# A two-layer graph network on one core: a new order for the first three and the last two graphs, and one seed of the last graph written straight into its own bank

## The chip, the cores and the metric

The kernel runs on one core of one Trainium2 chip. The metric is the device time of one execution in microseconds (us). PE (TensorE) does the matmuls, ACT (ScalarE), DVE (VectorE) and POOL (GpSimd) the elementwise work, SP (SyncE) issues every DMA. PSUM is used as eight banks of 128 partitions x 512 fp32 values, `bank0` to `bank7`.

## The reference, cut to what matters

64 graphs, each with `x` (256 nodes x 512 features) and an adjacency `adj` (256x256), all fp32:

```python
h = relu(layernorm(x))                                   # layer 0
agg = (adj @ h) / rowsum(adj)
x = x + relu(concat(h, agg) @ W.T)                       # W is 512 x 1024
h = relu(layernorm(x))                                   # layer 1
Xw = h @ Wv + bv
e = leaky_relu((Xw @ aw[:512]).T + Xw @ aw[512:] + ab)   # 256 x 256
T = adj * exp(e);  T = T / rowsum(T)
x = x + relu(h @ Wk[0] + bk[0] + (T @ h) @ Wk[1] + bk[1] + (T @ T @ h) @ Wk[2] + bk[2])
```

## The kernel before, in words

Matrix products are done with fewer block products than usual: Strassen-like sums of half-size blocks are prepared first (`wide` for W of layer 0, `main` for the rest, with steps numbered 1 to 7), and each block product is a 128x128 by 128x256 matmul, two recorded matmuls per fp32 block. All matmuls go through line 459, all bank-to-SBUF copies on ACT through line 471, the DVE sums with a bank operand through 474 and 477 (in `wide` through 652), the sums without one through `pool_op`, 420 on DVE or 422 on POOL.

One graph goes through the stages prepare (layer norm, adjacency scaled by its row sums), prepared, wide, layer0, turn1 (second norm and two vectors `sj`, `si`), transition (T), moved, once (T @ h), inner, turned1 and outer (the output). Stages of several graphs overlap; from the third graph on a transposed copy is made through DRAM (`put`, line 380, and `get`, line 386), for the first graphs on PE (`flip_on_pe`, line 404).

**What sets the order.** Every operation is registered by `add(engine, cost, run, reads, writes)` (line 231). Its place is a number: graph x `TURN` (38.52) plus the entry of the table `AT` for its stage, in order of registration, counted from 0. The stages `first` and `weights` belong to no graph and take the bare number. `emit` (line 253) sorts by this number, and what one engine got is that engine's instruction order; an instruction whose inputs are late holds back all that follow on its engine. `cost` is handed to `note` (line 250), which does nothing. The suffixes `_0`, `_1`, `_2` name the first three graphs, `_late` and `_last` the last two; the graphs between use tables without a suffix. Below, "transition_0.6" is operation 6 of stage transition of graph 0.

Operations that matter later:

- `first`: 0 and 1 load the halves of graph 0's x; 6 to 9 load the four 512 KB blocks of W into `x2` to `x5` (line 784); 10 to 24 (even) transpose it on PE (line 796), two blocks for each; the odd ones copy to SBUF on ACT; 27 to 54 are the 28 DVE sums that make W's block forms (lines 812 and 814); 55 to 57 load graph 0's adjacency, graph 1's x and graph 1's adjacency (lines 342, 345).
- `wide`: its PE operations use a form of W each; wide_0.16 is the first DVE sum (line 652) on a product of graph 0.
- layer0: 4 to 14 are products and seeds; 15 and 16 (line 563) finish x. turn1: 0 to 7 the norm, 8 to 11 `sj` and `si` on DVE (line 677), 13 and 14 DVE transposes, 15 to 18 the four writes of them to DRAM.
- transition: 0 writes `sj` to DRAM (line 686), 1 reads it back as a row (line 687), 2 to 5 are leaky ReLU and exp on ACT (692, 695), 6 and 7 the product with adj and its sums on DVE (697), 8 and 9 the reciprocal, 10 and 11 the scaling on ACT (703), 12 and 14 the PE transposes (404), 13 and 15 their copies (410).
- inner: 0 (step 1), 1 (step 7), 4 (step 2) and so on multiply `zg` with Wk[2]'s forms `lq`.
- outer of the last graph runs `main` with `last`: p, r, d are banks 3, 4, 5, x and y banks 6 and 7. Steps 5, 1, 6, 7 sum into bank 3; after each of them DVE adds a bias and puts the result as a "seed" into another bank (line 474 or 477), on which steps 2, 3 and 4 go on. The seed of step 3 goes into the upper half of bank 4, and after step 2 ACT copies it to bank 7 (line 546); step 3 waits for that. Each finished quarter of the output is added to x (line 756) and written (line 758).

Of the kernel before, what the change touches and what calls it, by code (L numbers as in the profile page):

```python
# [11 lines left out]
AF = mybir.ActivationFunctionType  # L12
# [15 lines left out]
    "first": (-90.93, -53.23, -117.99, -108.94, -110.36, -116.23, -69.23, -51.75, -160.39, -107.21, -61.21, -22.37, -27.53, -12.34, -45.26, -1.78,  # L28
        -84.29, -28.27, -93.32, 13.37, -47.15, -20.43, -156.60, -71.50, -119.21, -46.84, -42.27, -129.45, -122.63, -61.71, -52.35, -32.94, -72.67,
        -62.56, -45.91, -151.57, -67.52, -60.72, 2.83, 15.02, -11.78, 19.40, 29.16, -47.95, -25.77, 48.23, -47.81, -32.81, -19.46, -48.89, 7.13,  # L30
        20.41, -32.63, 17.85, 10.53, -123.51, 5.76, 21.86),
    "inner": (105.13, 108.59, 106.23, 109.69, 109.89, 110.76, 112.05, 116.38, 111.97, 114.07, 117.47, 117.50, 122.79, 115.08, 117.06, 118.02, 137.51),
    "inner_0": (104.64, 107.10, 112.63, 109.63, 108.85, 109.21, 114.17, 115.99, 113.73, 110.41, 129.80, 114.72, 119.54, 110.75, 113.34, 116.02,
        129.11),
    "inner_1": (110.70, 112.22, 111.49, 112.47, 113.83, 115.31, 114.08, 115.66, 116.33, 115.18, 129.29, 117.74, 125.91, 116.89, 117.80, 117.56,
        155.03),
    "inner_2": (110.70, 111.20, 111.98, 113.63, 111.78, 114.32, 114.94, 116.88, 115.46, 116.06, 116.42, 116.98, 124.86, 117.74, 119.04, 117.57,
        134.35),
    "inner_last": (336.53, 367.29, 384.59, 334.45, 391.73, 454.67, 522.64, 533.37, 408.60, 470.37, 504.02, 528.93, 492.30, 558.54, 500.07, 537.12,
        580.23),  # L40
    "inner_late": (108.31, 111.76, 110.85, 113.85, 112.13, 112.69, 114.05, 114.68, 123.33, 115.61, 145.82, 118.27, 122.89, 115.88, 119.11, 120.04,
        164.89),
    "layer0": (20.96, 24.01, 34.26, 38.15, 36.30, 37.47, 38.90, 39.56, 40.20, 40.90, 41.49, 42.16, 41.93, 42.79, 43.22, 43.47, 44.25),
    "layer0_0": (43.30, 43.73, 40.76, 63.15, 62.04, 64.91, 63.69, 65.17, 65.45, 66.86, 68.03, 68.37, 68.31, 69.19, 69.32, 68.45, 68.75),
    "layer0_1": (31.27, 36.57, 33.97, 43.43, 46.13, 48.74, 46.62, 49.21, 46.86, 49.66, 48.01, 49.83, 48.25, 48.79, 50.67, 49.93, 50.78),
    "layer0_2": (24.88, 28.19, 23.22, 43.47, 37.98, 37.09, 39.47, 39.22, 40.19, 41.59, 40.57, 42.04, 42.75, 43.10, 41.23, 47.00, 44.33),
    "layer0_last": (50.01, 57.68, 33.91, 60.79, 65.66, 66.71, 68.41, 66.94, 69.01, 68.24, 69.91, 69.27, 70.80, 71.03, 72.73, 71.96, 75.23),
    "layer0_late": (15.20, 21.71, 35.30, 40.31, 42.84, 48.47, 47.89, 49.57, 47.98, 49.76, 48.90, 49.94, 48.91, 50.48, 49.70, 51.70, 50.97),
    "loads": (-59.49, -45.29),
    "loads_2": (-40.12, -36.06),  # L50
    "loads_last": (-58.91, -32.90),
    "loads_late": (-54.89, -85.13),
    "moved": (89.04, 92.46, 93.17, 93.66, 94.15, 98.50),
    "moved_0": (94.08, 96.00, 97.15, 96.58),
    "moved_1": (87.63, 93.34, 94.62, 96.56, 97.69, 105.10),
    "moved_2": (88.68, 91.56, 91.23, 91.84, 96.02, 106.19),
    "moved_last": (139.05, 163.46, 205.96, 169.91),
    "moved_late": (96.66, 97.72, 100.63, 101.15),
    "once": (61.25, 64.00, 75.09, 75.88, 94.29, 95.59, 94.96, 99.41, 98.19, 98.63, 100.80, 101.23, 101.56, 100.30, 105.75, 103.00, 102.97, 103.89,
        106.56, 107.35, 108.14),  # L60
    "once_0": (85.34, 86.38, 98.69, 87.50, 93.62, 98.46, 98.58, 97.73, 98.58, 100.34, 100.69, 102.20, 101.36, 98.56, 103.24, 103.33, 102.27, 102.98,
        104.33, 105.25, 108.42),
    "once_1": (57.59, 69.48, 97.24, 96.50, 95.31, 95.58, 95.01, 99.66, 97.26, 98.27, 100.29, 102.15, 100.46, 102.80, 103.34, 105.40, 106.15, 108.95,
        105.21, 110.88, 111.17),
    "once_2": (63.41, 76.25, 69.81, 96.68, 93.52, 97.13, 93.09, 100.30, 100.95, 102.43, 103.05, 103.30, 102.21, 102.90, 103.59, 109.13, 104.57,
        107.39, 107.54, 109.97, 115.46),
    "once_last": (102.80, 135.83, 148.28, 162.89, 124.41, 120.18, 145.98, 187.50, 162.35, 203.89, 212.10, 233.57, 187.89, 213.05, 223.02, 232.11,
        256.18, 243.42, 255.25, 267.18, 321.27),
    "once_late": (66.99, 88.23, 64.29, 90.92, 99.96, 101.37, 100.45, 101.19, 101.37, 101.90, 105.80, 107.13, 110.31, 103.81, 110.60, 107.37, 105.93,
        106.50, 106.70, 107.63, 115.35),  # L70
    "outer": (108.93, 110.52, 122.87, 129.37, 114.22, 117.68, 119.41, 120.07, 120.70, 121.57, 122.87, 123.53, 124.60, 125.46, 126.33, 126.99, 127.62,
        130.65, 131.52, 132.19, 128.92, 131.95, 134.55, 134.99, 141.93, 152.31, 138.02, 140.19, 162.69, 160.60, 164.14, 164.93),
    "outer_0": (94.35, 98.74, 125.62, 106.70, 102.31, 116.27, 117.12, 118.24, 117.50, 117.80, 121.31, 124.46, 124.00, 125.58, 126.52, 126.71, 128.22,
        128.87, 132.65, 133.67, 128.80, 131.21, 134.36, 137.61, 140.55, 144.44, 136.33, 141.49, 160.49, 160.36, 163.66, 166.03),
    "outer_1": (106.89, 111.90, 118.77, 120.53, 108.75, 117.68, 119.18, 119.21, 120.59, 120.95, 123.23, 122.93, 123.75, 126.63, 126.70, 127.43,
        127.87, 128.74, 130.19, 132.33, 130.44, 131.84, 139.05, 141.13, 148.79, 152.10, 133.45, 136.68, 160.29, 160.80, 164.22, 166.72),
    "outer_2": (108.39, 111.96, 127.91, 140.81, 108.40, 121.23, 123.19, 121.63, 124.71, 125.64, 126.27, 125.65, 128.28, 128.68, 129.01, 128.91,
        131.04, 134.92, 135.36, 134.36, 132.23, 135.69, 137.94, 142.17, 143.69, 152.32, 138.41, 140.22, 150.30, 161.80, 164.00, 171.57),
    "outer_last": (498.02, 668.57, 694.33, 671.17, 577.46, 581.61, 593.26, 565.87, 615.19, 623.17, 650.49, 630.60, 695.13, 726.44, 735.87, 784.68,
        743.01, 838.42, 843.34, 796.04, 842.17, 761.60, 792.50, 751.08, 788.70, 811.00, 818.37, 858.45, 840.44, 876.17, 953.80, 975.74, 975.14,  # L80
        1020.56, 876.63, 891.60, 907.44, 875.80, 872.80),
    "outer_late": (109.06, 117.31, 186.73, 151.51, 116.15, 116.30, 119.62, 120.47, 120.01, 120.90, 123.12, 123.38, 129.10, 132.52, 132.66, 129.78,
        134.77, 139.77, 140.44, 139.50, 141.87, 144.49, 145.13, 158.57, 188.07, 200.85, 150.49, 152.04, 158.47, 232.29, 199.18, 211.96),
    "prepare": (-43.06, -41.74, -40.72, -35.30, -36.24, -28.72, -27.19, -23.45, -19.80, -15.93, -24.36, -24.98, -20.94, -12.75, -1.76, -2.28, -14.82,
        -13.49, -12.68, -12.13, -11.03, -11.58, -0.32, 1.04, 0.48, 2.14, 1.59),
    "prepare_0": (-84.88, -53.30, -37.93, -28.72, -22.39, -78.13, -74.85, -6.63, -18.20, -7.49, -144.71, -60.68, -137.04, -101.76, -12.58, -21.22,
        -26.38, -2.11, -10.47, 18.05),
    "prepare_1": (-15.07, -17.62, -8.06, -6.13, -0.14, -1.19, -0.63, 0.54, 7.75, 18.63, -38.44, -18.61, -14.54, 4.73, 16.46, 7.28, 12.55, 17.02,
        21.02, 19.33),
    "prepare_2": (-29.75, -29.48, -28.24, -24.75, -27.62, -28.40, -18.19, -16.40, -14.88, -13.91, -13.33, -6.35, -3.17, 8.62, 7.51, 7.67, -7.58,  # L90
        -2.32, -3.08, -1.25, 10.97, -0.12, 9.45, 9.24, 6.13),
    "prepare_last": (-41.49, -47.42, -40.82, -36.74, -38.40, -39.37, -36.21, -27.41, -24.96, -22.93, -7.95, -5.29, -3.53, 0.52, -2.38, -0.41, -8.95,
        -8.06, 0.10, 9.16, 6.05, -3.83, 2.64, 1.68, 2.00, -1.88, -3.02),
    "prepare_late": (-34.61, -47.32, -24.01, -19.75, -22.44, -22.19, -20.22, -19.93, -12.10, -16.22, -28.31, -35.76, -26.99, -25.62, -0.63, -19.64,
        -11.10, -13.45, -13.43, -9.03, -11.19, -7.53, -0.35, -0.68, -1.43, -1.97, 0.33),
    "prepared": (-7.18, 5.89, 11.28),
    "prepared_0": (8.94, 11.22, 28.01, 44.28),
    "prepared_1": (30.89, 31.47, 31.46, 30.86),
    "prepared_2": (13.00, 25.59),
    "prepared_last": (9.25, 6.90, 2.69),  # L100
    "prepared_late": (-3.13, 0.63, 10.23),
    "transition": (52.39, 56.28, 64.51, 63.42, 65.05, 63.97, 66.52, 67.12, 67.73, 68.04, 68.40, 68.92, 69.51, 71.25, 71.80, 70.70, 72.35),
    "transition_0": (74.09, 74.94, 85.61, 86.74, 87.55, 87.22, 90.49, 90.24, 90.60, 91.41, 91.25, 92.03, 91.61, 91.53, 93.51, 94.10),
    "transition_1": (53.67, 62.32, 65.20, 65.85, 69.15, 70.70, 67.77, 67.85, 67.92, 69.48, 74.55, 74.24, 70.13, 70.67, 70.52, 71.81, 77.46),
# [5 lines left out]
    "turn1_1": (49.63, 49.70, 50.51, 51.10, 51.13, 51.73, 53.03, 53.21, 53.66, 53.93, 58.29, 58.86, 64.81, 54.56, 54.30, 58.29, 62.00, 58.02, 61.54),  # L110
    "turn1_2": (43.11, 45.01, 43.93, 52.82, 53.16, 53.50, 49.16, 51.40, 52.03, 52.20, 54.30, 57.90, 58.08, 51.29, 54.09, 59.58, 56.28, 52.52, 56.97),
    "turn1_last": (75.41, 78.96, 77.17, 178.47, 184.64, 192.21, 86.15, 103.27, 80.59, 81.84, 83.21, 85.38, 104.79, 93.44, 122.16, 115.84, 150.29,
        115.69, 113.30),
    "turn1_late": (42.12, 48.32, 51.63, 53.75, 53.93, 54.07, 55.81, 56.33, 52.09, 61.66, 67.71, 71.29, 74.60, 66.82, 79.34, 84.95, 89.16, 79.81,
        97.48),
    "turned1": (100.59,),
# [155 lines left out]
def gnn_two_layers(ctx: ExitStack, tc: tile.TileContext, x, adj, w0, wv, bv, aw, ab, wk, bk, out):  # L272
    nc = tc.nc
# [702 lines left out]
```

## Time and profile before

| | us |
|---|---|
| median of 3 runs | 2547.44 (2547.05 to 2548.68) |
| the profiled execution's own time | 2545.75 |
| its span | 2544.0 |
| PE busy in it | 2509.1 (99%), 12412 matmuls |
| DVE, ACT, POOL busy | 1653.6, 1322.6, 1560.1 |
| DMA moved | 296.85 MB, mean 117 GB/s |
| mean granted PE clock | 0.997 |

The profile has several views. The table by stretches gives for each window of time the busy time of every engine, the clock that PE was granted (1.00 is full speed) and the DMA load. The timeline lists instructions in order of time, merged where several alike follow one another: start, duration, engine, line of the kernel, what it writes and reads, how many, and in square brackets the idle time before it and who ended that. The chain is the sequence of work that ended last, followed back from the end. A matmul's end is modelled, so the distance between starts says more than one duration.

### The profile page before, as it was taken

What the parts mean: (1) busy time and instruction counts of PE and PEld (TensorE: products, weight loads), DVE (VectorE), ACT (ScalarE), POOL (GpSimd) and SP (SyncE); (2) the same over time, 40 slices, a digit from 0 to 9 for tenths busy, and PEclk for the clock granted to TensorE, in tenths of its full rate; (3) what the DMA queues carried; (4) which work ended last, traced back from release to release, by engine and by line L of the source; (5) the groups of instructions that cost most, each with busy time, mean ns of one, the idle gap of its engine ahead of it and who ended that gap; (6) DMA issues with size and microseconds to landing.
All of it is one profiled execution on the core that took longest, in us unless ns stands there. A gap on an engine that the chain in (4) does not pass through costs nothing.

```text
span 2544.0 us, 39950 instructions
## 1 busy us (share of the span) xinstructions
PE 2509.1 (99%) x12412; PEld 2213.5 (87%) x12412; DVE 1653.6 (65%) x4099; ACT 1322.6 (52%) x3551; POOL 1560.1 (61%) x2475
## 2 busy tenths in 40 slices
PE   7899999999999999999999999999999999999998
PEld 5688888888888888888888888888888888888887
DVE  5766666666666666666666666666666666666654
ACT  7455555555555555555555555555555555555521
POOL 5565666666666666666666656656666666666640
PEclk9999999999999999999999999999999999999999
DMA  4354454454454454444444544544544544544421
GB/s 150 85 131 117 113 129 120 115 125 117 117 129 112 115 135 110 119 125 120 120 120 116 127 121 111 128 122 113 127 119 117 126 113 116 135 112 115 110 71 44
DMA packets 574571, 296.85 MB, mean 117 GB/s; under 512 B 417171, under 2 KB 540819, under 8 KB 574358
## 3 DMA queue, kind: packets, MB, share of 16 engines
q1 hardware_dynamic: 574358, 294.31, 47.0%
q8 instruction: 98, 1.61, 0.3%
q14 instruction: 115, 0.94, 0.1%
HBM read 162.80 MB, written 131.40 MB: 116 GB/s over the span
## 4 chain that ended last, share of the span: by engine, by line
PE 96%; DVE 1%; DMA 1%; SPq 0%; ACT 0%; issue 0%; POOL 0%; DVEq 0%; ACTq 0%; POOLq 0%
PE bank L459 96%; DMA dh<-turned 0%; DMA x<-in_L_gnn_W_dram 0%; DMA l<-in_L_gnn_Wv_dram 0%; SPq L380 0%; DVE bank L474 0%; DVE zg L420 0%; DMA out_dram<-x 0%; DVE z L677 0%; DVE turned L376 0%; PE bank L404 0%; ACT h1n L362 0%; DVE bank L652 0%; SPq L345 0%; DVE zg L474 0%
## 5 line engine op out<-in xcount | busy, mean ns | idle before, releaser
L459 PE MATMUL bank<-l,s 128*128 128x256 f32 x3292 | 876.9, 380 | 6.6 <-ACT bank L546 2.1
L459 PEld LDWEIGHTS bank<-l,s 128*128 128x128 f32 x3292 | 611.6, 191 | 91.4 <-issue 5.1
L471 ACT COPY stg<-bank 128x256 f32<-128x256 f32 x944 | 337.2, 371 | 524.8 <-PE bank L459 203.6
L459 PE MATMUL bank<-l,zg 128*128 128x256 f32 x1820 | 469.2, 380 | 1.6 <-ACT mz L471 0.9
L459 PE MATMUL bank<-lq,zg 128*128 128x256 f32 x1792 | 447.8, 380 | 3.7 <-DVE zg L474 1.3
L459 PEld LDWEIGHTS bank<-lq,zg 128*128 128x128 f32 x1792 | 340.4, 190 | 51.1 <-DVE zg L474 2.3
L459 PEld LDWEIGHTS bank<-l,zg 128*128 128x128 f32 x1820 | 337.2, 191 | 42.3 <-ACT mz L471 1.7
L422 POOL TENSOR_TENSOR zg<-zg 128x256 f32<-128x256 f32 x183 | 131.7, 733 | 353.8 <-ACT zg L471 347.4
L652 DVE TENSOR_TENSOR bank<-bank,stg 128x256 f32<-128x256 f32 x505 | 210.3, 428 | 202.1 <-PE bank L459 138.8
L459 PE MATMUL bank<-l,h0t 128*128 128x256 f32 x1008 | 291.3, 382 | 1.6 <-DVE q L652 0.8
L422 POOL TENSOR_TENSOR s<-h0t,s 128x256 f32<-128x256 f32 x315 | 234.0, 743 | 0.5
L459 PEld LDWEIGHTS bank<-l,h0t 128*128 128x128 f32 x1008 | 197.4, 197 | 26.8 <-DVE q L652 2.3
L677 DVE SCALAR_TENSOR_TENSOR z<-h1n,v_sb 128x512 f32<-128x512 f32 x256 | 211.9, 828 | 13.1 <-ACT h1n L368 4.4
L459 PE MATMUL bank<-l,h1t 128*128 128x256 f32 x784 | 203.3, 381 | 1.3 <-DVE lo L477 1.0
L471 ACT COPY qf<-bank 128x256 f32<-128x256 f32 x128 | 47.6, 372 | 285.3 <-DVE qf L474 250.3
L422 POOL TENSOR_TENSOR qf<-qf 128x256 f32<-128x256 f32 x122 | 113.5, 930 | 117.4 <-DVE qf L474 117.4
L459 PEld LDWEIGHTS bank<-l,h1t 128*128 128x128 f32 x784 | 153.1, 197 | 20.1 <-DVE lo L477 2.3
L563 DVE SCALAR_TENSOR_TENSOR x<-bank,x 128x512 f32<-128x512 f32 x254 | 165.4, 686 | 2.7 <-PE bank L459 1.9
L459 PE MATMUL bank<-q,sa 128*128 128x256 f32 x512 | 152.9, 380 | 2.3 <-DVE bank L474 1.6
L459 PE MATMUL bank<-qf,st 128*128 128x256 f32 x512 | 152.6, 380 | 0.8 <-DVE qf L420 0.7
L422 POOL TENSOR_TENSOR s<-h0t 128x256 f32<-128x256 f32 x189 | 143.5, 773 | 9.3 <-ACT h0t L410 6.6
L422 POOL TENSOR_TENSOR hf<-h1n,hf 128x256 f32<-128x256 f32 x124 | 91.3, 736 | 89.9 <-PE bank L459 89.9
(178 smaller groups left out, 4418.3 us busy)
## 6 DMA issues: line engine op xcount, KB each, us to landing
dh<-turned SPq DMA_DIRECT2D x500, 128.0 KB, 3.3
h1t<-dh SPq DMA_DIRECT2D x64, 512.0 KB, 3.8
x<-in_x_dram SPq DMA_DIRECT2D x63, 512.0 KB, 4.6
out_dram<-x SPq DMA_DIRECT2D x63, 512.0 KB, 3.1
h0t<-dh SPq DMA_DIRECT2D x61, 512.0 KB, 4.0
a<-in_adj_dram SPq DMA_DIRECT2D x64, 256.0 KB, 4.3
dan<-turneda SPq DMA_DIRECT2D x248, 64.0 KB, 1.9
raw<-dan SPq DMA_DIRECT2D x62, 256.0 KB, 2.7
```

What stands on the lines that cost most here:

```text
L422: add("POOL", cost, lambda: getattr(nc.gpsimd, f)(to, p, q), reads, writes)
L459: nc.tensor.matmul(ps, lhs, rhs, start=start, stop=True, skip_group_check=True)
L471: add("ACT", 0.37, lambda: nc.scalar.copy(dst, bank[b][:, cols]), [f"bank{b}"], dkeys)
L563: add("DVE", 0.75 if sums else 0.69, lambda c=c: nc.vector.scalar_tensor_tensor(t[:, c, :], bank[banks[1 + c]], 0.0, t[:, c, :], op0=ALU.m ...
L652: add("DVE", 0.43, lambda f=f, to=to, x=x, y=y: getattr(nc.vector, f)(to, x, y), pbk + [k], tok)
L677: add("DVE", 0.79, lambda s=s, c=c: nc.vector.scalar_tensor_tensor(scr.rearrange("p c n -> p (c n)"), h[:, c, :], 1.0, v_sb[:, s, :], op0= ...
```

## The change

Three things are edited. First, the tables for `first`, `weights` and all stages with the suffixes `_0`, `_1`, `_2`, `_late` and `_last` get new numbers; the tables without suffix, `TURN` and `SHIFT` stay. Second, in `main` with `last` the seed of step 3 is written by DVE to bank 7 at once, and ACT's copy is gone (the list for `outer_last` has one entry less, so its entries from 26 on move down by one). Third, three `cost` values of ACT operations with a row sum are larger. The changed file has one line more, so its line numbers above 528 are larger by one (and back by the removed lines where those lie).

```diff
-    "first": (-90.93, -53.23, -117.99, -108.94, -110.36, -116.23, -69.23, -51.75, -160.39, -107.21, -61.21, -22.37, -27.53, -12.34, -45.26, -1.78,
...
-        20.41, -32.63, 17.85, 10.53, -123.51, 5.76, 21.86),
+    "first": (-259.48, -286.32, -474.02, -306.06, -368.19, -123.55, -208.45, -206.90, -285.80, -358.64, -231.88, -223.99, -262.31, -253.20, -282.95,
...
+        -276.54, -348.24, -262.55, -227.12, -429.92, -242.38, -165.16, -204.46, -43.14, -159.19, -203.45, -533.74, -116.49),
...
-    "inner_0": (104.64, 107.10, 112.63, 109.63, 108.85, 109.21, 114.17, 115.99, 113.73, 110.41, 129.80, 114.72, 119.54, 110.75, 113.34, 116.02,
...
+    "inner_0": (98.57, 102.21, 100.10, 107.77, 100.97, 104.63, 106.76, 110.88, 111.13, 110.63, 117.33, 113.91, 121.76, 112.18, 114.67, 115.25,
...
-    "layer0_1": (31.27, 36.57, 33.97, 43.43, 46.13, 48.74, 46.62, 49.21, 46.86, 49.66, 48.01, 49.83, 48.25, 48.79, 50.67, 49.93, 50.78),
+    "layer0_1": (34.16, 43.08, 27.22, 49.21, 44.98, 42.29, 45.82, 43.73, 45.96, 44.95, 46.62, 46.27, 46.99, 48.02, 48.22, 46.63, 46.67),
-    "transition_0": (74.09, 74.94, 85.61, 86.74, 87.55, 87.22, 90.49, 90.24, 90.60, 91.41, 91.25, 92.03, 91.61, 91.53, 93.51, 94.10),
+    "transition_0": (61.61, 65.18, 81.16, 82.84, 81.31, 85.36, 81.78, 83.07, 83.76, 84.73, 86.36, 86.51, 87.63, 85.30, 87.79, 89.93),
-    "turn1_0": (63.74, 65.84, 65.81, 68.40, 69.22, 69.25, 71.74, 72.28, 72.38, 74.92, 75.31, 75.59, 82.08, 77.96, 80.29, 88.16, 87.40, 86.65, 74.22),
+    "turn1_0": (58.31, 59.35, 59.68, 51.67, 52.08, 54.45, 63.43, 64.26, 65.60, 66.04, 68.44, 75.22, 78.15, 72.44, 74.52, 69.08, 68.95, 66.00, 71.90),
+    "outer_last": (1243.02, 1439.80, 1512.86, 1480.80, 1226.84, 1301.09, 1315.52, 1219.36, 1349.21, 1359.08, 1383.14, 1432.38, 1433.64, 1561.25,
+        1601.21, 1443.35, 1680.73, 1813.96, 1828.85, 1469.59, 1857.20, 2155.25, 1899.21, 1897.11, 2010.73, 2223.60, 2337.58, 2160.45, 2297.51,
+        2379.16, 2412.28, 2624.78, 2409.02, 2274.51, 2290.95, 2365.82, 2125.75, 1980.72),
...
-                add("ACT", 0.66, lambda c=c: nc.scalar.activation(h[:, c, :], s[:, c, :], AF.Identity, accum_out=sm[:, c : c + 1]),
+                add("ACT", 0.82, lambda c=c: nc.scalar.activation(h[:, c, :], s[:, c, :], AF.Identity, accum_out=sm[:, c : c + 1]),
...
-            add("ACT", 0.74, lambda c=c: nc.scalar.activation(h[:, c, :], s[:, c, :], AF.Square, bias=sm[:, c : c + 1], accum_out=sq[:, c : c + 1]),
+            add("ACT", 0.91, lambda c=c: nc.scalar.activation(h[:, c, :], s[:, c, :], AF.Square, bias=sm[:, c : c + 1], accum_out=sq[:, c : c + 1]),
...
         p, r, d = banks[:3]
+        e, cols = (banks[4], lo) if last else (r, hi)
...
-        plus(bank[r][:, hi], [f"bank{r}"], p, lo, s12, keys[1:])
+        plus(bank[e][:, cols], [f"bank{e}"], p, lo, s12, keys[1:])
         step(7, p, lo, terms)
         if last:
-            x, y = banks[3:]
+            x = banks[3]
             plus(bank[x][:, lo], [f"bank{x}"], p, lo, s21[:, 1], keys[1:])
             last(1, hi, x, lo)
             plus(bank[d][:, lo], [f"bank{d}"], p, lo, s21[:, 0], keys[:1])
             step(2, r, lo, terms)
-            add("ACT", 0.37, lambda: nc.scalar.copy(bank[y][:, lo], bank[r][:, hi]), [f"bank{r}"], [f"bank{y}"])
             last(0, lo, r, lo)
-            step(3, y, lo, terms)
-            last(0, hi, y, lo)
+            step(3, e, cols, terms)
+            last(0, hi, e, cols)
             step(4, d, lo, terms)
             last(1, lo, d, lo)
...
-            add("ACT", 0.45, lambda c=c: nc.scalar.activation(an[:, c, :], a[:, c, :], AF.Identity, accum_out=dg[:, 0, c : c + 1]),
+            add("ACT", 0.61, lambda c=c: nc.scalar.activation(an[:, c, :], a[:, c, :], AF.Identity, accum_out=dg[:, 0, c : c + 1]),
```

## The prediction

> **What bounds the kernel now.** I first read the page's table of the span in 40 slices: PE is at nine tenths or more in all of them but the first two and the last. So the time is PE's work plus PE's idle time, and the table by stretches says where the idle time lies. The columns are the stretch, its length, the busy time of PE, PEld, DVE, ACT and POOL with their instructions, the clock granted to PE, the DMA share and GB/s.
>
> ```profile
> 10.00:20.00 10.00, 6.68 (x32) 5.69 (x33) 7.35 (x23) 9.44 (x28) 2.25 (x6) 1.00 1.09 345
> 20.00:30.00 10.00, 9.90 (x53) 8.13 (x52) 7.89 (x17) 7.81 (x22) 7.16 (x12) 0.83 1.01 321
> 70.00:80.00 10.00, 5.70 (x22) 3.61 (x22) 7.18 (x19) 6.10 (x17) 5.87 (x10) 0.90 0.47 92
> 80.00:90.00 10.00, 7.93 (x33) 6.47 (x32) 6.84 (x22) 3.60 (x9) 0.78 (x1) 0.59 0.56 149
> 2000.00:2100.00 100.00, 100.00 (x505) 89.29 (x504) 67.16 (x165) 55.11 (x148) 62.85 (x101) 1.00 0.49 120
> 2530.00:2540.00 10.00, 7.91 (x30) 6.35 (x29) 1.94 (x5) 0.36 (x1) 0.00 (x0) 0.83 0.08 26
> ```
>
> From 2000 to 2100 PE never stops, at full clock. PE is idle for 24.7 us in the first 120 us, for one wait of 0.5 between 120 and 2400, and for some 2.1 at the very end; two of these places also show a lowered clock (0.59 and 0.83). The change touches only these two ends, so about 25 us and some clock are all that it can win. The chain of waits shows the end (start, length, engine, what):
>
> ```profile
> 2527.85 4.57 PE bank L459 x20
> ...
> 2534.08 0.37 ACT bank L546
> 2534.49 6.29 PE bank L459 x20
> ```
>
> Two lots of 20 matmuls of one shape: 4.57 us ahead of ACT's copy, 6.29 behind it. PE's timeline says why:
>
> ```profile
> 2534.49 1.13 PE L459 MATMUL bank<-l,s 128*128 128x256 f32 x4 [2.09 <-ACT bank L546]
> 2535.46 1.82 PE L459 MATMUL bank<-l,h1t 128*128 128x256 f32 x4
> 2537.07 1.91 PE L459 MATMUL bank<-l,zg 128*128 128x256 f32 x4
> ```
>
> PE stands 2.09 us for the copy, and soon after four matmuls take 1.82 and 1.91 instead of 1.03. At the head the largest gap belongs to graph 0's transition; PE's timeline there:
>
> ```profile
> 76.09 0.70 PE L459 MATMUL bank<-l,s 128*128 128x256 f32 x2 [1.04 <-DVE q L652]
> 77.53 0.44 PE L404 MATMUL bank<-ident,an 128*128 128x128 f32 x2 [0.74 <-ACT an L703]
> 79.62 0.69 PE L404 MATMUL bank<-ident,an 128*128 128x128 f32 x2 [1.65 <-ACT an L703]
> 80.77 1.22 PE L459 MATMUL bank<-tt,h1n 128*128 128x128 f32 x4 [0.46 <-ACT tt L410]
> 81.78 1.92 PE L459 MATMUL bank<-l,s 128*128 128x256 f32 x4
> 85.31 1.19 PE L459 MATMUL bank<-l,s 128*128 128x256 f32 x2 [1.61 <-ACT stg L471]
> ```
>
> **The sum is made against the profiled execution, 2545.75 us (span 2544.0); the median is 1.69 above it, which I add at the end.** Which instruction passes which follows from sorting the table numbers, old and new, engine by engine.
>
> **Tail: -3.5.** Step 3's seed goes straight to bank 7, so ACT's copy (0.37) and the wait for it (2.09) go. No new wait follows: the seeds of steps 3 and 4 are two of the DVE additions of 0.78 us for two, made right behind step 7, while step 2's ten matmuls keep PE busy for 2.15. Without the wait I take the last 20 matmuls at the 4.57 of the lot before: another 1.72. What comes next late is the output: in SP's new order three of the four 128 KB writes start within the last 1.2 us, where they were spread before. Two more of them ahead of the last cost at most 256 KB at the 345 GB/s of the row 10 to 20, 0.74; at least nothing, as that load is only 0.08 here. I take 0.3. -2.09 - 1.72 + 0.3 = -3.51 (bounds -3.8 to -3.1). The other new places of the last two graphs meet a PE that waits 0.62 us for a seed two times; I take 0, and up to 1 either way.
>
> A rule stands beside this row. The Trainium skill, "TensorE: Matmul & The Clock Gate", section "Part 1: The HAM clock gate", says that PE falls to half rate after an idle window of about 3.4 us. The rows show lowered rates after a wait of 2.09, so the measurement decides; by the rule as written no clock would come back anywhere, the tail would give -1.8, the transition below -2.75, and the whole sum 2542.9 instead of 2539.7.
>
> **Graph 0's transition: -4.25 (0 to -8.5).** The five waits shown sum to 1.04 + 0.74 + 1.65 + 0.46 + 1.61 = 5.50. Between 80.77 and 88 five groups run slow: 1.22 for 0.61, 1.92 for 1.03, 1.19 for 0.60, 1.06 for 0.61 twice; 2.99 in all. Upper end 8.5. What moves: on SP the read of `row` is behind one write of `turned` before (issued at 63.50, the read at 63.94) and ahead of it after; on DVE the product with adj (transition_0.6 and 7) passes layer0_1.15 and 16; on ACT the scaling (10 and 11) passes graph 1's squares; wide_2.31 and 34 pass graph 1's norm. Each of these shortens the path to `an`, but what it passes (graph 1's finish of layer 0) is needed soon after by the same idle PE, and SP's issue of graph 3's adjacency now stands behind three writes; it was needed at 76.6 and would land at about 71 (the writes end near 66, plus a landing of 4.6). I take half, because what is moved forward is about as much as what is moved back.
>
> **Start: +1.3 (0 to +2.4).** SP now begins with graph 1's x (512 KB), and W's blocks are issued second, fourth, sixth and seventh; before they were first, third, fifth and seventh. Until the last block of W lands 3.0 MB are asked for, 2.75 before; 0.25 MB at 345 GB/s is 0.75 us. DVE's form list shows what hangs on it:
>
> ```profile
> 10.75 0.42 DVE L814 TENSOR_TENSOR l<-q,zg 128x256 f32<-128x256 f32 x1 [10.75 <-ACT zg L471]
> ...
> 13.72 0.42 DVE L814 TENSOR_TENSOR q<-bank,l 128x256 f32<-128x256 f32 x1 [0.35 <-PE bank L796]
> ...
> 25.70 0.75 DVE L652 TENSOR_TENSOR bank<-bank,stg 128x256 f32<-128x256 f32 x2
> ```
>
> Before, DVE starts at 10.75 on blocks that came first; after, its first form needs W's late blocks. Before, the first sum that reads a bank of PE's transposes started at 12.42; I put the new first one at 12.42 + 0.75, about 13.15. From 13.72 it did 26 instructions to 25.77, 0.463 each; 30 of them from 13.15 end at 27.0, against 25.70: +1.3. If this early list has slack it costs 0; if DVE loses its whole early start of 10.75 to 13.15, +2.4. POOL gets a combine of 2.37 us (weights.49) ahead of two small sums; its weight is issued 29th, some 8.2 MB into the loads, lands near 26 to 29 at 282 to 345 GB/s, and the sum behind it (wide_0.8) is used past 35: covered, 0. If it landed after 33, PE would wait.
>
> **Rest of the head: -1.25 (-5 to +2.4).** inner_0's step 2 now stands ahead of step 7, so some eight matmul groups instead of three cover `zg`, whose wait was 1.25 at 97.25: gone. Eleven other waits between 54 and 111 sum to 7.3; the reorder can halve or keep them, or add one as large as the largest of the head's, 2.3. I take them unchanged, since each engine's order moves some of their releasers up and some down. The new cost values go to a function that does nothing: 0. No matmul is added or taken away.
>
> Sum: -3.51 - 4.25 + 1.3 - 1.25 = -7.71; 2538.04, and with 1.69 **2539.7 us**.
>
> **Rivals.** *Given back in the head*: what passes is late, and what was passed is late next; the transition and zg waits only change their names. Tail and start alone: -3.51 + 1.3 = -2.21, 2545.2. For it: PE, DVE and ACT are all below 8 of 10 from 70 to 80, a chain of dependences rather than a busy engine. *All of it*: tail, the whole 8.5, 1.25, start free: -13.26, 2534.2. For it: the waits name single instructions of ACT that now stand earlier. *Slower, by the late start*: the loads of W share the bandwidth instead of queueing, so all 32 transposes come after 11.8 at 0.228 each (19 in 4.32), end at 19.1 instead of 15.4, and DVE's forms come 3.7 late; PE waits in short pieces from 20 to 40 and its clock stays at the 0.59 of the row 80 to 90: (0.83 - 0.59) x 10 = 2.4 and (1.00 - 0.59) x 10 = 4.1. 3.7 + 2.4 + 4.1 - 3.51 = +6.7, 2554.1. It decides once the head loses 8.6 us. Against it: PE takes W's first products only from 19.86, and W's last block is the seventh issue both times. *The seed does nothing*: bank 7's seed late, so a DVE wait replaces ACT's; 2532.44 to 2533.22 for two seeds against 2.15 of cover speaks against it, and the case falls into the first rival with 3.5 less, 2548.7.
>
> **How the numbers follow.** Forecast 0.48, all of it 0.18, given back 0.24 (the useless seed in it), slower 0.10. A difference of 0.2%, 5.1 us, is about what a measurement of this kernel can tell from no change: 2542.3 and 2552.5 are the borders. Faster 0.66, same 0.24, slower 0.10. The low end takes the second rival less half of the other head waits, 2534.2 - 3.6, about 2531; the high end the first rival with the start at +2.4 and one wait of 2.3 more, about 2549.
>
> **What would show it.** Tail: no wait of PE after step 2, the last 20 matmuls in about 4.6, no clock below 1.00 from 2530 on, the last write landing within 2.8 of the last sum. Transition: waits named `an`, `tt`, `stg` below 3 in sum and a clock over 0.8 from 70 to 90. Start: the first 652 sum at 27.0. Head: PE idle near 20 in the first 120 us. I am wrong if the idle time of the first 120 us is the same or more, or if the transition's clock stays at 0.6.

## The result, and the profile after

The changed kernel takes 2555.14 us (median of 9 runs, 2554.55 to 2557.23) against 2548.68 (9 runs, 2547.05 to 2550.48): a ratio of 1.0029, 95% interval 1.0020 to 1.0038. It is slower, and outside the range of the prediction. Its profiled execution has a span of 2552.7 us, 8.7 more than that of before. The traces lie further apart than the medians (6.46), because the profiled execution of before (2545.75) is 2.93 faster than its median and that of the changed kernel is at its median.

The changed file's table of places is one line longer, so all line numbers behind it are larger by one, and not only those above 528: its line 460 is line 459 of before, its 472 is 471, its 475 is 474. In c_seed, below, line 459 has become 522.

First the table by stretches of the changed kernel, with the columns as above (PE, PEld, DVE, ACT, POOL busy, clock, DMA share, GB/s):

```profile
10.00:20.00 10.00, 7.14 (x42) 5.84 (x40) 6.23 (x20) 8.65 (x27) 1.52 (x6) 1.00 1.06 363
20.00:30.00 10.00, 9.26 (x50) 5.92 (x49) 7.54 (x20) 8.93 (x30) 7.59 (x12) 1.00 0.90 252
70.00:80.00 10.00, 7.28 (x41) 5.24 (x41) 8.33 (x24) 8.11 (x24) 4.69 (x9) 1.00 0.22 34
80.00:90.00 10.00, 8.32 (x40) 6.69 (x40) 5.99 (x18) 4.07 (x11) 3.49 (x5) 1.00 0.75 197
2000.00:2100.00 100.00, 99.62 (x489) 87.80 (x488) 66.09 (x161) 52.28 (x141) 64.62 (x106) 1.00 0.46 114
2540.00:2550.00 10.00, 8.87 (x40) 7.57 (x40) 2.68 (x7) 0.00 (x0) 0.00 (x0) 1.00 0.05 17
```

The head and the tail did what was hoped for: more PE work in 70 to 90, clock 1.00 in every row. The row that matters is the dull one in the middle. From 2000 to 2100 PE now does 489 matmuls where it did 505, and it is no longer quite full (99.62). The count alone says little, since 100 us hold some two and a half graphs and windows cut them differently: before has 493 from 2100 to 2200, with PE busy throughout. The page's 40 slices hide it: nine tenths before, nine tenths after.

The chain of waits of the changed kernel ends in one run of 40 matmuls, with no ACT in it:

```profile
2540.45 8.89 PE bank L460 x40
2549.36 0.42 DVE x L757
```

To place the loss I lined up both traces at the same event, the first matmul of the form `bank<-q,sa` of each graph (all times in us):

| event | before | after | difference |
|---|---|---|---|
| graph 6 | 260.95 | 251.53 | -9.42 |
| graph 20 | 800.29 | 795.96 | -4.33 |
| graph 40 | 1570.76 | 1574.06 | +3.30 |
| graph 61 | 2379.75 | 2390.70 | +10.95 |
| last group of matmuls | 2540.17 | 2548.73 | +8.56 |
| end of the span | 2544.0 | 2552.7 | +8.7 |

So in these traces the head won 9.42, the end of the kernel won 2.39, and the 55 graphs between lost 20.37: each takes 38.89 instead of 38.52, steadily, 0.37 us per graph. The tables of these graphs weren't edited, and on every engine their instructions stand in the same order as before.

The place in each graph, first before, then after (timelines of all engines, cut to the same spot of a middle graph):

```profile
495.67 0.41 DVE L474 TENSOR_TENSOR qf<-bank,mz 128x256 f32<-128x256 f32 x1
...
496.26 0.42 DVE L474 TENSOR_TENSOR qf<-bank,qf 128x256 f32<-128x256 f32 x1 [0.18 <-PE bank L459]
496.43 1.03 PE L459 MATMUL bank<-l,zg 128*128 128x256 f32 x4
496.63 0.43 DVE L474 TENSOR_TENSOR bank<-bank,p 128x256 f32<-128x256 f32 x1
496.72 0.37 ACT L471 COPY qf<-bank 128x256 f32<-128x256 f32 x1 [4.26 <-DVE qf L474]
...
497.29 0.59 PE L459 MATMUL bank<-q,sa 128*128 128x256 f32 x2
```

```profile
527.31 0.41 DVE L475 TENSOR_TENSOR qf<-bank,mz 128x256 f32<-128x256 f32 x1
...
527.83 0.37 ACT L472 COPY qf<-bank 128x256 f32<-128x256 f32 x1 [3.73 <-PE bank L460]
...
528.06 1.03 PE L460 MATMUL bank<-l,zg 128*128 128x256 f32 x4
...
528.30 0.42 DVE L475 TENSOR_TENSOR qf<-bank,qf 128x256 f32<-128x256 f32 x1 [0.58 <-ACT qf L472]
528.65 0.42 DVE L475 TENSOR_TENSOR bank<-bank,p 128x256 f32<-128x256 f32 x1
...
529.21 0.67 PE L460 MATMUL bank<-q,sa 128*128 128x256 f32 x2
```

ACT's copy `qf<-bank` (inner.10) and DVE's sum `qf<-bank,qf` (inner.11) both read bank 6. Before, DVE goes first and ACT waits for it (4.26, ended by DVE). After, ACT goes first and DVE waits for ACT (0.58). ACT's copy can wait, since PE doesn't need its result soon; DVE's sum can't, because the seed that DVE writes next, `bank<-bank,p`, is what PE's `q,sa` needs. In the changed kernel, where `qf<-bank,qf` is late, the seed starts 1.34 us behind `qf<-bank,mz` instead of 0.96, and `q,sa` starts 1.15 behind the `l,zg` group instead of 0.86. That is 0.29, and the first group after the stall is 0.08 longer (0.67 for 0.59).

The programs' instruction lists say the same with their waits (engine, line, what it waits for):

```
before: ACT L471 qf<-bank    waits for DVE        DVE L474 qf<-bank,qf  waits for PE, POOL
after:  ACT L472 qf<-bank    waits for PE         DVE L475 qf<-bank,qf  waits for ACT, POOL
```

So the two reads of one bank are put in sequence in both programs, the one put down first ahead of the other. The Trainium skill, "PSUM — Partial Sum Buffer", section "PSUM bank collisions raise a hardware error", says that two engines must be kept apart on one bank and quadrant of partitions, reads against reads included. No run here lets two reads overlap; the traces agree as far as they go: ACT starts 0.04 after DVE's end before (496.68, 496.72), and DVE 0.10 after ACT's after (528.20, 528.30).

Which is put down first is decided in `emit`, and not by the place numbers of the two:

```python
for i in sorted(range(len(self.ops)), key=lambda i: self.ops[i][3]):
    queues.setdefault(self.ops[i][0], []).append(i)
...
    for e, queue in queues.items():
        while heads[e] < len(queue) and self.ops[queue[heads[e]]][2] <= done:
```

The engines are walked in the order in which each first turns up in the sorted list. (An engine puts down all that it can before the next one has its turn.) With the old tables that is SP (-160.39), PE (-156.60), DVE (-151.57), ACT (-144.71), POOL (-117.99). With the new numbers of the first graph it is ACT (-583.97), DVE (-580.40), SP, POOL, PE. **Theory (pair order):** this exchange of ACT and DVE turned the pair in all graphs. **Rival (state at entry):** the graphs enter the middle 9 us earlier and settle into another rhythm, whatever the walk.

### The profile page after: what moved, and what is told of

Same layout as the page of the kernel before. It is cut to its first block, busy times and chain, and to the rows that moved or that the text cites. A ratio compares the mean times of both kernels' runs of the same rounds, so it can differ in the third digit from the quotient of the medians.

```text
span 2552.7 us, 39968 instructions
## 1 busy us (share of the span) xinstructions
PE 2513.0 (98%) x12412; PEld 2205.3 (86%) x12412; DVE 1646.8 (65%) x4099; ACT 1322.6 (52%) x3550; POOL 1561.5 (61%) x2475
## 4 chain that ended last, share of the span: by engine, by line
PE 95%; DMA 1%; DVE 1%; POOL 1%; ACT 1%; issue 1%; SPq 0%; DVEq 0%; POOLq 0%; ACTq 0%
PE bank L460 95%; DMA dtt<-turneda 0%; DMA x<-in_L_gnn_W_dram 0%; POOL s L423 0%; DMA raw<-dtt 0%; DMA raw<-dan 0%; DVE bank L475 0%; PE bank L797 0%; ACT h1n L363 0%; SPq L381 0%; ACT h1n L369 0%; PE bank L405 0%; POOL sa L423 0%; POOL q L423 0%; POOL l L776 0%
```

## The experiments

**a_rot: the changed kernel, engines walked as before.** Walking them DVE, ACT, SP, POOL, PE gives a program with the same instructions and the same waits, so of the whole walk only DVE ahead of ACT matters.

```diff
-        queues = {}
+        queues = {e: [] for e in ("SP", "PE", "DVE", "ACT", "POOL")}
```

> The changed kernel, with one line of emit set so that the five engines are walked in the order that they had before (SP, PE, DVE, ACT, POOL); in the changed kernel ACT comes ahead of DVE. Every engine's own instruction order stays that of the changed kernel. Theory (pair order): the middle graphs go back from 38.89 to 38.52 us each, because the sum and the copy that both read bank 6 are again put down as DVE first, ACT second; 56 graphs times 0.366 is 20.4, so 2555.1 - 20.4 = 2534.7, with up to 2 either way from other pairs in the head and the tail. Rival (state at entry): the graphs enter the middle some 9 us earlier and in another phase, and settle into a slower pattern whatever the walk of the engines is: 2555, 38.89 per graph.

Measured: 2534.87 (ratio to before 0.9945, 0.9933 to 0.9957). The graphs take 38.52 again, but for one of 38.84; graph 6 stands at 251.54, as in the changed kernel, and graph 58 at 2254.75, still 9.43 ahead of before. The same spot in its trace has the old order:

```profile
795.02 0.42 DVE L475 TENSOR_TENSOR qf<-bank,qf 128x256 f32<-128x256 f32 x1 [0.18 <-PE bank L460]
...
795.39 0.43 DVE L475 TENSOR_TENSOR bank<-bank,p 128x256 f32<-128x256 f32 x1
795.48 0.37 ACT L472 COPY qf<-bank 128x256 f32<-128x256 f32 x1 [4.26 <-DVE qf L475]
```

The theory holds, the rival falls: the graphs enter as early as in the changed kernel and keep the old rhythm.

**b_rot: the kernel before, engines walked as after.**

```diff
-        queues = {}
+        queues = {e: [] for e in ("ACT", "DVE", "SP", "POOL", "PE")}
```

> The kernel before, with the engines walked as in the changed kernel (ACT, DVE, SP, POOL, PE); nothing else. Theory (pair order): 38.89 per graph from the third graph on, 2548.7 + 20.4 = 2569, with up to 3 more from pairs in the head and the tail. Rival (state at entry): 2548.7, 38.52 per graph.

Measured: 2565.82 (1.0072, 1.0058 to 1.0086), 38.89 per graph. The mechanism is there, but the sum is 3 below the expectation. At graph 61 the trace is 21.09 behind before, at the last matmuls only 19.06: in the tail this walk wins about 2 us, which the last experiment explains. The rest of the 3 lies within what the heads of two executions differ (below).

**a_pair and b_pair: that pair alone.** a_pair is the changed kernel with the copy put down behind the sum in the graphs 3 to 61; b_pair is the kernel before with the sum put down behind the copy.

```diff
         plus(*t2, bx, lo, *b11)
+        if 2 < g < G - 2:
+            plan.ops[-2][2].add(len(plan.ops) - 1)
```

```diff
         plus(*t2, bx, lo, *b11)
+        if 2 < g < G - 2:
+            plan.ops[-1][2].add(len(plan.ops) - 2)
```

> The changed kernel with one thing only: in graphs 3 to 61 ACT's copy inner.10 is put down after DVE's sum inner.11, both of which read bank 6; the walk of the engines stays ACT first. Theory, in its narrow form (this pair alone costs the 0.366 per graph): 38.52 per graph and 2534.7, up to 2 either way. If other pairs turned round by the walk matter as well: between 2537 and 2553. Rival (state at entry): 2555.

> The kernel before with one thing only: in graphs 3 to 61 DVE's sum inner.11 is put down after ACT's copy inner.10. Theory, narrow form: 0.366 for each of 59 graphs, 2548.7 + 21.5 = 2570, up to 2 either way. Rival (state at entry): 2548.7, since nothing moves in the head.

Measured: a_pair 2534.05 (0.9944, 0.9932 to 0.9957), the same as a_rot; b_pair 2572.69 (1.0095, 1.0081 to 1.0109), with 38.89 per graph. So the one pair carries the whole loss of the middle; what the other pairs cost there, if anything, is below what these runs can tell. b_pair lies 2.7 above its expectation, and where that comes from isn't settled: its trace is 2.53 behind before at graph 6 already, where nothing was changed, loses 21.29 from there to graph 61, and 2.32 more behind it. A head differs by some us from one execution to the next: in the six traces of this study with the old head graph 6 starts at 260.95 to 264.55, with before the earliest of them, and in the five with the new head at 249.95 to 253.92. So the 9.42 of the line-up is a low figure for what the head won.

**c_seed, c_tail, c_head, best: the parts of the change, engines walked as before.** c_seed has the old places and the seed in bank 7; c_tail adds the new places of the last two graphs; c_head has the new places of the head alone; best has the new head and the seed, with the old places of the last two graphs. (Most of the head's tables can't be taken alone: the orders of two engines would wait for each other in a circle. So the new head was run as a whole, and what each of its tables is worth stays open.)

```diff
+AT.update({
...
+})
-        queues = {}
+        queues = {e: [] for e in ("SP", "PE", "DVE", "ACT", "POOL")}
```

> All places of the kernel before, and of the change only the seed that DVE writes straight to bank 7 (its place in the list is the old one, ACT's copy and its entry are gone). The walk of the engines is the old one. If the tail step of the prediction is right (2.09 of wait and 1.72 of lowered clock, less 0.3 for bunched output): 2548.9 - 3.5 = 2545.4, within 1.5. The trace of a_rot has the last 40 matmuls in 8.89 where the kernel before needs 12.93 for them, which would make it -3.9. Rival (the gain of the tail needs the new places of the last two graphs): no change, 2548.9.

> The seed and the new places of the last two graphs; the head and the weights as before, the walk of the engines the old one. From the distance between a_rot and before, which is -9.1 us at graph 61 and -11.7 at the last matmul: -2.6, 2546.3. If it is above c_seed, the new places of the last two graphs lose about 1.3 by themselves; if they gain, it is below c_seed.

> The new places of the first three graphs and of the weights, the last two graphs and the seed as before, the walk of the engines the old one. From the distance at graph 6: -9.4, 2539.5, with 38.52 per graph. The prediction's own terms for the head (-4.25 + 1.3 - 1.25 = -4.2) would give 2544.7; its rival (all of it) 2539.

> The new places of the head, the seed written straight to bank 7, the old places of the last two graphs, the walk of the engines the old one. If head and seed add up: 2548.9 - 9.4 - 3.9 = 2535.6, and about 1.3 below a_rot as run here if the new places of the last two graphs lose; equal to a_rot if they don't.

| | median | to before, 2548.56 | interval of the ratio |
|---|---|---|---|
| c_seed | 2545.57 | -3.0 | 0.9980 to 0.9998 |
| c_tail | 2546.36 | -2.2 | 0.9982 to 1.0000 |
| c_head | 2537.26 | -11.3 | 0.9944 to 0.9972 |
| best | 2533.24 | -15.3 | 0.9927 to 0.9953 |

Head and seed add up (-11.3 and -3.0 make -14.3; together they give -15.3, within the runs' spread), and best has the lowest median of the study, though its interval overlaps those of a_rot and a_pair. c_head and best lie 2.2 and 2.4 below what was expected of them, since the expectation took the head from the trace of before, whose head is an early one. The chain of waits of c_seed ends without ACT:

```profile
2531.56 8.89 PE bank L522 x40
2540.47 0.42 DVE x L819
```

From the start of these 40 matmuls to the last DVE sum it takes 8.91 us; before it was 2540.80 - 2527.85 = 12.95. The new places of the last two graphs win nothing: from graph 61 to the last group c_tail gains 2.38 on before and c_seed 4.02, so they cost about 1.6 in the traces. The traces of a_rot and best, with the new head, show the same (2.58 and 4.04); the medians of c_tail and c_seed (0.8 apart) can't settle it, and c_tail's interval reaches 1.

**b_tailpair: another pair of the same kind.** In b_rot ACT's copy of the seed, the very copy that the change removes, no longer held PE up. In the kernel before it waits for a DVE sum that only reads the same bank 4. Here the kernel before has the copy put down ahead of that sum, and keeps it.

```diff
             add("ACT", 0.37, lambda: nc.scalar.copy(bank[y][:, lo], bank[r][:, hi]), [f"bank{r}"], [f"bank{y}"])
+            copied = len(plan.ops) - 1
             last(0, lo, r, lo)
+            plan.ops[copied + 1][2].add(copied)
```

> The kernel before, with one thing only: in the last graph ACT's copy of step 3's seed is put down ahead of the DVE sum last(0, lo), which reads the same bank 4; the copy and its bank 7 stay. If the wait of 2.09 us came from that pair's order, as b_rot's trace suggests (there the copy runs 0.7 us after step 2 begins to end, and the last 40 matmuls take 8.89 instead of 12.93), the whole gain of c_seed comes without its edit: 2548.6 - 3 to 4, so about 2545, and the same as c_seed's 2545.6 within 1. If the copy's own place behind step 2 was the cause, as the prediction had it, at most the 0.76 of the DVE sums is won: 2547.8.

Measured: 2544.32 against 2547.88 in the same series (0.9986, 0.9977 to 0.9995): -3.6, as much as c_seed within the intervals. The timeline around the copy, before and in b_tailpair:

```profile
2532.44 0.76 DVE L474 TENSOR_TENSOR bank<-bank,lo 128x256 f32<-128x256 f32 x2 [4.74 <-PE bank L459]
2533.24 0.75 DVE L756 SCALAR_TENSOR_TENSOR x<-bank,x 128x256 f32<-128x256 f32 x2
...
2534.08 0.36 ACT L546 COPY bank<-bank 128x256 f32<-128x256 f32 x1 [13.70 <-DVE x L756]
```

```profile
2534.20 0.36 ACT L546 COPY bank<-bank 128x256 f32<-128x256 f32 x1 [10.81 <-PE bank L459]
...
2535.45 0.77 DVE L474 TENSOR_TENSOR bank<-bank,lo 128x256 f32<-128x256 f32 x2 [4.74 <-PE bank L459]
```

```profile
2530.86 8.89 PE bank L459 x40
```

In the kernel before, DVE's read of bank 4 stands behind two seeds, which wait for the end of step 7, and PE finishes step 7 only behind step 2; so the copy comes after all 20 matmuls. In b_tailpair it waits for PE, runs while PE still works on step 7, and the chain (third fence) has the 40 matmuls without a gap. The copy itself was not the cost; its place behind DVE's read was.

## Why the prediction was wrong, point by point

- **The step that failed is the first:** "The change touches only these two ends, so about 25 us and some clock are all that it can win." The orders were compared engine by engine, "from sorting the table numbers", and the middle came out equal. Equal orders on every engine aren't an equal program: the order *between* two engines that read one bank also counts, and the new places at the head turned it. The middle, which the sum leaves at nothing, lost 0.37 us per graph, 20.37 over 55 graphs, more than both ends won. None of the rivals had the middle in it, so even the slower one (2554.1, close to the 2555.14) was right by accident. Nor could the signs of being wrong show it: PE's idle time of the first 120 us fell from 24.7 to 21.4 and the transition's clock rose to 1.00, as hoped.
- **Slower, by the late start: refuted.** DVE's form list in the changed kernel:

```profile
13.70 0.42 DVE L815 TENSOR_TENSOR q<-bank,l 128x256 f32<-128x256 f32 x1 [13.70 <-ACT l L472]
...
24.26 0.76 DVE L653 TENSOR_TENSOR bank<-bank,stg 128x256 f32<-128x256 f32 x2 [0.28 <-PE bank L460]
```

  It begins at 13.70 (put at 13.15), yet the first product sum starts at 24.26, 1.4 ahead of before and 2.7 ahead of the 27.0 forecast. The pitch of 0.463 that I carried over contained waits and slow sums (0.89 to 1.06) that the new order mostly lacks; here 30 instructions from 13.70 to 24.26 take 0.352 each.
- **Transition: right in kind, put too low.** The waits at this place in the changed kernel:

```profile
72.46 0.44 PE L405 MATMUL bank<-ident,an 128*128 128x128 f32 x2 [0.69 <-DVE tt L411]
72.73 0.60 PE L460 MATMUL bank<-l,s 128*128 128x256 f32 x2
73.57 0.70 PE L460 MATMUL bank<-l,s 128*128 128x256 f32 x2 [0.24 <-ACT stg L472]
74.10 0.61 PE L460 MATMUL bank<-tt,h1n 128*128 128x128 f32 x4
74.55 0.60 PE L460 MATMUL bank<-l,s 128*128 128x256 f32 x2
76.55 0.67 PE L460 MATMUL bank<-l,s 128*128 128x256 f32 x2 [1.41 <-ACT stg L472]
```

  2.34 us instead of 5.50, and `tt,h1n` in 0.61 instead of 1.22: 3.16 of wait and most of the 2.99 of slow matmuls, where I took half of both. For the whole head, up to graph 6, PE's busy time for the same 1112 matmuls (before, then after):

```profile
0.00:260.95 260.95, 235.81 (x1112) 194.01 (x1113) 169.10 (x415) 148.16 (x408) 154.78 (x243) 0.97 0.47 122
```

```profile
0.00:251.53 251.53, 229.13 (x1112) 189.69 (x1113) 161.19 (x415) 147.35 (x408) 154.46 (x243) 1.00 0.49 127
```

  The same matmuls take 6.68 less, and PE's idle time falls from 25.14 to 22.40, by 2.74. The 6.68 is the clock: the rows of before with 0.83, 0.90 and 0.59 fall short of full speed by 1.7 + 1.0 + 4.1 = 6.8 us, and in the changed kernel all three show 1.00. I had the head at -4.25 + 1.3 - 1.25 = -4.2; it is -9.4 in the trace, and c_head's runs give -11.3. The mis-sized term is the clock: I took half of the 2.99 of one place and nothing for the row 20 to 30, though the prediction shows its 0.83. With its whole transition and a free start the rival *all of it* (-13.26) was nearest to what the ends are worth (-14.0 in a_rot's runs).
- **inner_0's wait, -1.25: wrong.** PE still waits 1.08 for `zg` at 89.56, for a DVE sum of line 421 again. More matmuls ahead of it didn't cover it.
- **Tail, -3.5: right in size, wrong in cause.** c_seed gives -3.0, the trace -4.04 without the output; the lowered clock came back with the wait. The output ends 2.92 after the last DVE sum in the changed kernel and 2.78 before, so the bunched writes cost some 0.14 in these two traces (put at 0.3). But I took the wait as the copy's own; b_tailpair shows that it was the order of two readers.
- **By the rule on the clock gate** that the prediction weighed, the tail would have given -1.8, or -2.1 without the 0.3 for the output; the trace of c_seed gives -4.04 without the output, so here the rows were the better guide.
- **The rest.** The `cost` values go to a function that does nothing; no run changes them alone. With the middle undone (a_rot) the change is worth -14.0, 2534.9: faster, inside the range and 4.8 below the forecast.

## What to carry to other kernels

When a table or a list decides an order, compare the programs with their waits, across engines, and not only each engine's own order: where two engines read one PSUM bank, look which read is put first. The one whose result is needed later should be the second: in the middle graphs that was ACT's copy, at the end of the last graph DVE's sum. A loss of 0.37 us in each of 55 turns hardly shows in a window of the profile (99.62 for 100.00) and is larger than everything won at the ends, so line up two traces at one event per turn before reading anything else. Here the fix is a fixed walk of the engines (or the pair's order written down), and with it the change is faster by 0.55% (a_rot), and best by 0.60%.

## What the runs showed of the hardware that was not expected

PE's clock in the head goes with the order of the work. From 80 to 90 us it is 0.51 to 0.59 in all six traces with the old head, and 1.00 in all five with the new one, although single waits of up to 1.41 us remain there. From 20 to 30 us it differs even between traces with the same new head (1.00 in after, 0.95 in a_rot, 0.92 in a_pair). Which length or share of idle time turns it isn't settled by these runs. One graph in the middle of the changed kernel (34) came 0.35 later than its neighbours' pace; its cause stays open.
